# Rows of a and c from transposes of their columns, multiplied by g1 in VectorE's eviction; sums of squares of a as variances of these rows; positions redrawn

## The chip, the cores and the metric

The kernel runs on one core of one Trainium2 chip. The metric is the device time of one execution in microseconds, the median of three runs. A core has five engines with queues of their own, each worked through in order: TensorE (PE; its weight loads are shown as PEld), VectorE (DVE), ScalarE (ACT), GpSimd (POOL) and SyncE (SP, which issues the DMAs here).

## The reference

Two graph layers over 32 graphs of 512 nodes with 128 features. `adj` is sparse: about one entry in sixteen, and the diagonal.

```python
# layer 0: x1 = LN(x + Dinv (adj + I) Dinv (x W) + bias)
# layer 1, for each graph:
m_j = x1 @ W1[:D]                      # "a" in the kernel, centred over its features
m_i = x1 @ W1[D:]                      # "c" (with b1, centred)
pre = m_j[:, None, :] + m_i[:, :, None] + b1   # one row of 128 per pair of nodes (i, j)
msg = gelu(layernorm(pre) * g1 + be1)          # exact gelu
agg = einsum("bijo,bij->bio", msg, adj)
upd = layernorm(concat(x1, agg) @ W2 + b2) * g2 + be2
out = LN(x1 + upd)
```

With rows a and c centred, the sum of squares of a pair's row, which its layernorm needs, is sum(a^2) + sum(c^2) + 2 a.c. Only pairs with a non-zero entry in `adj` matter, and the kernel finds and computes just these.

## The kernel before

Everything named here is inside `sparse_path`. A batch is one graph, B = 32. Nodes lie in C = 4 chunks of 128, so `adj` has 16 blocks of 128x128. For each batch the kernel makes, per block and row, a list of the neighbours, and then works through 20 *units* (t, q): t = 0 to 3 are the first places of the lists, four units each, t = 4 and 5 the rest ("shared" places), two units each. A unit gathers the rows of its pairs with one-hot matmuls (`pairs`, into `u` in PSUM), adds the other row (`sums`, VectorE, L896; not for t >= 4), applies gelu with the pair's factor as scale (`messages`, ScalarE, L929), multiplies one-hot weights by `adj` (`weights`, GpSimd, L912 and L916, tile `sw`) and sums into `agg` (`aggregate`, TensorE, L943 and L953).

Around the units stand helpers that prepare the next batch and finish the last, written as generators whose steps end at `yield`:

- `layer0`: loads (`xs`, `a_nat`, `own_w`), layer 0, x1 and its transpose `x1t`; then `pat`, `pct` (L381, L383: the columns of a and c), `asq`, `csq`, `at`, `ct` out of them on ScalarE, the sums of squares `psq`, `pcs` on TensorE, and `key`, the 512x512 variances with a mask for absent edges: matmuls `pv` (L415, L416) and one VectorE eviction for each of four row chunks (L410). Last, the diagonal's own values: `own_p`, and `own_v` (L427).
- `lists` (VectorE, L519 and L523), `more` (L593, L596, L599), `factors`, `counts` (`over`, `count`, `count_h`, then `po` on TensorE, L634), `spots` (`up_to`, `pj`, `sj`), `sending` (`pl` on TensorE, `sent` on ScalarE, L686), `picks` (`rank` L706, `kept`, `picked` on VectorE, `r_s` on GpSimd): which neighbours, their variances, the overflow of long lists. `idx_d`, `idx_ds`, `sd_d`, `sd_ds` go out to DRAM and come back as `raw` and `sd_rows`; `raw` becomes the one-hot `s` (VectorE, L832) and its transpose `mt` (a transposing DMA, L840).
- `parts`: rows of a and c times g1 (`pac`, matmuls against `w1g`), copied to `ac` by ScalarE, b1's part added by GpSimd, and c split into three bf16 parts `c3`.
- `own_edges`, `finish` (`agg_sb`, `pu`, layernorms, the store).

The order of everything is written out by hand, in `PLAN`: for each step of each helper a position in half units, relative to the first unit of its batch; 40 positions are one batch, and -30 is 30 half units ahead. In the main loop each engine's instructions stand in the order in which the program issues them (the pairs of two units at even units, the aggregation of two units at odd ones, the steps of a position between). Before the first unit the framework's scheduler orders them. The transient PSUM tiles share one pool `ps` of three banks (`bank(...)`): a fourth tile waits until the engine that reads the first has done so.

Of the kernel before, what the change touches and what calls it, by code (L numbers as in the profile page):

```python
# [8 lines left out]
F32 = mybir.dt.float32  # L9
# [3 lines left out]
AF = mybir.ActivationFunctionType  # L13
ALU = mybir.AluOpType
# [4 lines left out]
P = 128  # L19
# [8 lines left out]
PAD = 4  # L28
NEG = -1e30
DEV = 12  # L30

PLAN = {
    "layer0": [-43, -41, -39, -39, -38, -37, -36, -34, -34, -33, -32, -31, -30, -30, -29, -28, -27, -27, -27, -27, -26, -24, -20, -18, -16, -3],
    "lists": [-26, -26, -25, -24, -23, -20, -19, -19, -18, -18, -14, -13, -13, -13, -12, -12, -12, -11, -11, -10, -10],
    "parts": [-20, -14, -12, -11, -6, -5, -4, -4, -4],
    "factors": [-12, -11, -10, -8, -7, -7, -7, -6, -5],
    "more": [-26, -25, -12, -10, -10, -10, -8, -7, -6, -6, -6, -5, -5, -5, -5, -5, -5, -5],
    "counts": [-3, -3, -2, -2, -2],
    "own_edges": [7, 18, 22, 30],
    "spots": [-2, -1, 0, 2, 3, 4, 6, 7, 7, 7],  # L40
    "sending": [8, 9, 9, 9, 9, 9, 9, 9, 9, 9, 9, 9, 9, 9, 9, 9, 9],
    "picks": [10, 12, 12, 14, 15, 18, 20, 20, 20, 20, 22, 23],
    "finish": [43, 44, 45, 50, 53, 55, 55, 60, 62, 69, 70, 79, 80],
}


def bcast(ap, n):

    return ap.unsqueeze(1).to_broadcast([ap.shape[0], n, ap.shape[-1]])
# [16 lines left out]
def sparse_path(ctx, tc, x, adj, w0, b0, w1, b1, g1, be1, w2, b2, g2, be2, out, most, flag):  # L66
# [37 lines left out]
    ident = const.tile([P, P], F32, name="ident")  # L104
# [1 line left out]
    ident_h = const.tile([P, P], BF16, name="ident_h")  # L106
    nc.vector.tensor_copy(ident_h, ident)
    ones = const.tile([P, P], F32, name="ones")
    nc.gpsimd.memset(ones, 1.0)

    stri = const.tile([P, P], BF16, name="stri")
    nc.gpsimd.memset(stri, 1.0)
# [33 lines left out]
    own = slice(0, C * C, C + 1)  # L146
# [12 lines left out]
    eps_t = const.tile([P, 1], F32, name="eps_t")  # L159
# [17 lines left out]
    bmean = const.tile([P, 1], F32, name="bmean")  # L177
    nc.vector.tensor_scalar(bmean, bsum, 1.0 / D, None, ALU.mult)
    b1c_col = const.tile([P, 1], F32, name="b1c_col")
    nc.vector.tensor_sub(b1c_col, b1_col, bmean)  # L180

    b1g = const.tile([P, D], F32, name="b1g")
    nc.vector.scalar_tensor_tensor(b1g, rows["b1"], bmean, rows["g1"], ALU.subtract, ALU.mult)
    w1g = const.tile([P, 2, D], F32, name="w1g")
    nc.vector.tensor_tensor(w1g, w1c, bcast(rows["g1"], 2), ALU.mult)


    parts = node.tile([P, 3, D], F32, tag="f0", name="be_parts")
# [66 lines left out]
    def bank(key):  # L255
        return ps.tile([P, 512], F32, tag="ps", name=key)
# [10 lines left out]
    def layer0(b):  # L267

        st = state[b] = {}
# [13 lines left out]
        pt = transposed(xs, f"x_{b}")  # L283
        yield
        for mc in range(C):
# [8 lines left out]
            pt = bank(f"pa_{b}_{mc}")  # L294
# [61 lines left out]
        pt = bank(f"pconv_{b}")  # L356
# [25 lines left out]
        pc = bank(f"pct_{b}")  # L382
        nc.tensor.matmul(pc, w1c[:, 1, :], x1t, start=True, stop=True)  # L383
        yield
        asq = node.tile([P, N], F32, tag="t1", name=f"asq_{b}")
        nc.scalar.activation(asq, pa, AF.Square)
        csq = node.tile([P, N], F32, tag="t3", name=f"csq_{b}")
        nc.scalar.activation(csq, pc, AF.Square, bias=b1c_col)
        yield
        at2 = node.tile([P, N], F32, tag="t0", name=f"at2_{b}")  # L390
        nc.scalar.activation(at2, pa, AF.Copy, scale=2.0)
        ct = node.tile([P, N], F32, tag="t2", name=f"ct_{b}")
        nc.scalar.activation(ct, pc, AF.Identity, bias=b1c_col)
        yield
        pa = bank(f"psq_{b}")
        for q in range(C):
            nc.tensor.matmul(pa[:, q : q + 1], asq[:, q * P : (q + 1) * P], ones[:, :1], start=True, stop=True)
# [10 lines left out]
        for q in range(C + 1):  # L408
            if q:
                nc.vector.scalar_tensor_tensor(  # L410
                    key[:, q - 1, :], pt, a_sum[:, q - 1 : q], c_sum, ALU.add, ALU.add
                )
# [18 lines left out]
    def parts(b):  # L431

        st = state[b]
        x1t = st["x1t"]

        ac = node.tile([P, C, 2, D], F32, tag="ac", name=f"ac_{b}", bufs=2)
        c3 = node.tile([P, 3, C, D], BF16, tag="c3", name=f"c3_{b}", bufs=2)
        for h in range(C // 2 + 1):
            if h:
                part = ac[:, 2 * h - 2 : 2 * h, :, :]  # L440
                nc.scalar.copy(part, pt.rearrange("p (c k d) -> p c k d", k=2, d=D))
            if h < C // 2:
                pt = bank(f"pac_{b}_{h}")
                for c in range(2):
                    n0 = (2 * h + c) * P
                    nc.tensor.matmul(
                        pt[:, 2 * c * P : 2 * (c + 1) * P], x1t[:, n0 : n0 + P], w1g, start=True, stop=True
                    )
            yield
        rest = ac[:, :, 1, :]  # L450
        nc.gpsimd.tensor_tensor(rest, rest, bcast(b1g, C), ALU.add)
# [8 lines left out]
        st["ac"], st["c3"], st["own"] = ac, c3, own_u  # L460

    def own_edges(b):

        st = state[b]
        var, u = st["own_v"], st["own"]
        nc.gpsimd.tensor_scalar(var, var, 0.0, 1.0 / D, ALU.max, ALU.mult)
# [81 lines left out]
    def factors(b):  # L548

        st = state[b]  # L550
        n_r = SLOTS * 2 * C * C
        sd = small.tile([P, n_r], F32, tag="sd", name=f"sd_{b}", bufs=1)
        by_c = sd.rearrange("p (t h c q) -> p h q c t", t=SLOTS, h=2, c=C)
        top = st["top"].rearrange("p (q c) h t -> p h q c t", c=C)
        for h in BOTH:
            nc.gpsimd.tensor_scalar(by_c[:, h], top[:, h, :, :, :SLOTS], 0.0, None, ALU.max)
        yield
        nc.scalar.activation(sd, sd, AF.Sqrt, bias=eps_t, scale=1.0 / D)
# [140 lines left out]
    def picks(b):  # L699
# [38 lines left out]
        for q in range(C):  # L738
# [2 lines left out]
        nc.gpsimd.tensor_scalar(  # L741
            ve.rearrange("p (k c q) -> p k q c", k=SHARED, c=C),
            picked[:, 1, :].rearrange("p (k q c) -> p k q c", k=SHARED, c=C),
            1.0 / D,
            EPS,
            ALU.mult,
            ALU.add,
# [594 lines left out]
```

## Time and profile before

| | |
|---|---|
| median of 3 runs | 2945.51 us (2942.2 to 2951.59) |
| the profiled execution | 2950.83 us, its span 2949.1 us, mean granted TensorE clock 0.987 |
| TensorE busy | 2780.1 us, 94% of the span |
| ScalarE | 2540.1 us, 86% |
| VectorE | 2441.2 us, 83% |
| GpSimd | 2132.8 us, 72% |
| HBM over the span | 57 GB/s |

Busy time is the time covered by an engine's instructions; TensorE's are pipelined and their ends modelled, so the time from one start to the next says more there than the duration of one. A group's row gives its line, engine, shapes and count, then busy time and mean duration of one, then the idle time of the engine just before it and what ended it. Rows of waits give total, number and longest. The chain that ended last follows only the last few microseconds of this kernel and is no guide to the rest.

### The profile page before, as it was taken

The page shows a single profiled execution, that of the slowest core. Times are in us where ns is not written, and L with a number is a line of the kernel's source. Part 1 is how long each engine was busy: PE and PEld are TensorE (multiplying, and loading weights), DVE is VectorE, ACT ScalarE, POOL GpSimd, SP SyncE. Part 2 cuts the span into 40 slices and gives each one's busy share as a digit, 9 for nine tenths or more (in the row PEclk, how much of TensorE's full clock was granted, in tenths as well). Part 3 has the DMA queues.
Part 4 walks back from the last instruction along what each step waited for, and adds up shares of the span by engine and source line. Part 5 has one row for each costly group of instructions (what it writes and reads, how often), then busy time and mean ns, then how long its engine had stood idle before and what let it go on. Part 6 is the DMA issues. An engine that isn't in the chain of part 4 may idle for free. (4 is left out here: it accounts for less than half of the span.)

```text
span 2949.1 us, 96041 instructions
## 1 busy us (share of the span) xinstructions
PE 2780.1 (94%) x35393; PEld 2314.2 (78%) x35393; DVE 2441.2 (83%) x9834; ACT 2540.1 (86%) x7841; POOL 2132.8 (72%) x2621
## 2 busy tenths in 40 slices
PE   4999999999999999999999999999999999999996
PEld 2788878788787788787888787788787888787885
DVE  5788988888988888988889888889888889888882
ACT  2888998888888888988888988888989888888885
POOL 3677877777877767776777777778777778776765
PEclk7999999999999999999999999999999999999998
DMA  1444444444443444434444434444434444434442
GB/s 43 91 93 105 103 101 79 99 91 107 106 97 75 93 99 102 109 82 89 100 102 102 101 79 99 93 108 103 101 79 99 89 109 106 100 79 96 91 97 48
DMA packets 593022, 276.09 MB, mean 94 GB/s; under 512 B 456112, under 2 KB 576048, under 8 KB 592544
## 3 DMA queue, kind: packets, MB, share of 16 engines
q1 hardware_dynamic: 592320, 269.41, 42.3%
q8 instruction: 281, 4.60, 0.6%
q14 instruction: 197, 1.61, 0.2%
q0 software_dynamic: 224, 0.46, 0.1%
HBM read 155.45 MB, written 13.63 MB: 57 GB/s over the span
## 5 line engine op out<-in xcount | busy, mean ns | idle before, releaser
L929 ACT ACTIVATE m<-m,r 128x128 f32<-128x128 f32 x4096 | 1267.4, 393 | 39.3 <-DVE m L896 39.3
L912 POOL TENSOR_TENSOR sw<-mt,a_t 128x512 f32<-128x512 bf16 x512 | 617.6, 1220 | 132.3 <-DMA mt<-s 74.1
L896 DVE TENSOR_TENSOR m<-u,ac 128x1024 f32<-128x1024 f32 x512 | 607.0, 1207 | 14.3 <-PE u L877 14.1
L943 PE MATMUL agg<-m,sw 128*64 128x128 f32 x8192 | 514.0, 277 | 5.6 <-ACT m L929 5.0
L943 PEld LDWEIGHTS agg<-m,sw 128*64 128x64 f32 x8192 | 442.7, 137 | 92.0 <-issue 45.5
L869 PEld LDWEIGHTS <-s 64*128 64x128 bf16 x12288 | 365.7, 95 | 138.3 <-issue 63.7
L869 PE MATMUL u<-c,s 64*128 64x128 bf16 x12288 | 434.0, 218 | 13.3 <-DVE s L832 12.7
L686 ACT COPY sent<-pl 128x328 f32<-128x328 f32 x512 | 221.4, 432 | 126.4 <-PE pl L690 66.9
L916 POOL TENSOR_TENSOR sw<-mt,sent 128x512 f32<-128x512 bf16 x256 | 291.3, 1161 | 9.0 <-PE agg L953 6.3
L690 PE MATMUL pl<-a_t,sj 128*128 128x164 f32 x2048 | 293.6, 304 | 0.0
L690 PEld LDWEIGHTS pl<-a_t,sj 128*128 128x128 f32 x2048 | 285.6, 190 | 8.5 <-DVE y L367 8.2
L929 ACT ACTIVATE m<-u,r_s 128x128 f32<-128x128 f32 x1024 | 279.0, 378 | 6.2 <-PE u L890 5.9
L884 PE MATMUL u<-ac,sj 128*128 128x128 f32 x2048 | 273.7, 277 | 0.0
L884 PEld LDWEIGHTS u<-ac,sj 128*128 128x128 f32 x2048 | 263.5, 191 | 12.0 <-DVE a_t L596 5.1
L953 PE MATMUL agg<-m,sw 128*128 128x128 f32 x2048 | 247.5, 277 | 0.0
L953 PEld LDWEIGHTS agg<-m,sw 128*128 128x128 f32 x2048 | 238.7, 192 | 9.2 <-POOL own_u L476 7.9
L887 PE MATMUL u<-c,s 128*128 128x128 bf16 x3072 | 213.3, 219 | 0.0
L523 DVE FIND_INDEX8 idx<-top,key 128x8 uint32<-128x64 f32 x1024 | 210.1, 218 | 0.0
L593 DVE MATCH_REPLACE8 key<-top,key 128x64 f32<-128x64 f32 x1024 | 205.0, 207 | 0.0
L741 POOL TENSOR_SCALAR ve_s<-picked 128x32 f32<-128x32 f32 x32 | 7.9, 248 | 262.0 <-DVE picked L727 262.0
L887 PEld LDWEIGHTS <-s 128*128 128x128 bf16 x3072 | 193.6, 98 | 3.0
L877 PE MATMUL u<-be_d,sd_rows 64*128 64x512 bf16 x1024 | 195.7, 378 | 0.0
(212 smaller groups left out, 5739.6 us busy)
## 6 DMA issues: line engine op xcount, KB each, us to landing
raw<-idx_d SPq DMA_DIRECT2D x256, 256.5 KB
raw<-idx_ds SPq DMA_DIRECT2D x64, 513.0 KB
a_nat<-in_adj_dram SPq DMA_DIRECT2D x32, 1024.0 KB
sd_rows<-sd_d SPq DMA_DIRECT2D x768, 12.0 KB
xs<-in_x_dram SPq DMA_DIRECT2D x32, 256.0 KB
out_dram<-o_sb SPq DMA_DIRECT2D x32, 256.0 KB
sd_d<-sd_p SPq DMA_DIRECT2D x256, 12.0 KB
mt<-s SPq DMA_TRANSPOSE x192
```

The source lines that it names most:

```text
L523: nc.vector.max_index(idx[:, to, h, :], top[:, to, h, :], half(to, h))
L686: nc.scalar.copy(sent[:, n - 1], pt[:, : SHARED * WIDE].rearrange("p (k w) -> p k w", w=WIDE))
L690: nc.tensor.matmul(pt[:, k * WIDE : (k + 1) * WIDE], sj[:, n, k * P : (k + 1) * P], at[:, n, :], start=True, stop=True,)
L869: nc.tensor.matmul(pu[:, h, c, :], s[halved(h), c, q * P : (q + 1) * P], c3[halved(h), k, c, :], start=(c == 0 and k == 0), stop=False,)
L884: nc.tensor.matmul(pu[:, h, c, :], place, st["ac"][:, q_h, 0, :], start=(c == 0), stop=False)
L887: nc.tensor.matmul(pu[:, h, c, :], s[:, c, q_h * P : (q_h + 1) * P], c3[:, k, c, :], start=False, stop=False)
L896: nc.vector.tensor_tensor(u.rearrange("p h c d -> p (h c) d"), pu.rearrange("p h c d -> p (h c) d"), bcast(state[b]["ac"][:, q, 0, :], 2 * C),
L912: nc.gpsimd.tensor_tensor(sw, mt[:, :, q, :], st["a_t"][:, q, :, :P], ALU.mult)
L916: nc.gpsimd.tensor_tensor(sw, mt[:, :, q_h, :], a, ALU.mult)
L929: nc.scalar.activation(m[:, h, c, :], u[:, h, c, :], AF.Gelu, scale=r[:, k : k + 1])
L943: nc.tensor.matmul(agg[halved(h), c, :], sw[0][:, c, halved(h)], m[:, h, c, :], start=(begin and c == 0), stop=(end and c == C - 1),)
L953: nc.tensor.matmul(agg[:, c, :], sw[h][:, c, :], m[:, h, c, :], start=False, stop=(end and h == 1 and c == C - 1),)
```

## The change

The columns of a and c (`at`, `ct`), which the kernel makes anyway for the variances, are transposed on TensorE into `pac` (eight transposes of 128x128, two banks), instead of multiplying x1t by W1 x g1. VectorE multiplies each bank by g1 on its way to `ac`, and takes bn_stats of the four unscaled rows of a out of the same bank; their variance takes the place of `asq`, `psq` and `a_sum`. So that all fits without another instruction, `at` is scaled by 2 x KEY, `ones` holds KEY = 32, the g1 of a is divided by 2 x KEY, and 1/D becomes 1/(KEY x D) in three places: `key` is 32 times what it was. b1 is in `ct` already, so GpSimd's addition goes. `parts` loses three steps, and all of `PLAN` has new positions: `parts` begins at 17 of the batch before instead of 20, the first key at 18 instead of 14, `counts` at 39 to 46 instead of 37 and 38, `own_v` at 5 of its own batch instead of 37 of the one before.

```diff
+KEY = 32.0
 PLAN = {
-    "layer0": [-43, -41, -39, -39, -38, -37, -36, -34, -34, -33, -32, -31, -30, -30, -29, -28, -27, -27, -27, -27, -26, -24, -20, -18, -16, -3],
-    "lists": [-26, -26, -25, -24, -23, -20, -19, -19, -18, -18, -14, -13, -13, -13, -12, -12, -12, -11, -11, -10, -10],
-    "parts": [-20, -14, -12, -11, -6, -5, -4, -4, -4],
-    "factors": [-12, -11, -10, -8, -7, -7, -7, -6, -5],
-    "more": [-26, -25, -12, -10, -10, -10, -8, -7, -6, -6, -6, -5, -5, -5, -5, -5, -5, -5],
-    "counts": [-3, -3, -2, -2, -2],
-    "own_edges": [7, 18, 22, 30],
-    "spots": [-2, -1, 0, 2, 3, 4, 6, 7, 7, 7],
-    "sending": [8, 9, 9, 9, 9, 9, 9, 9, 9, 9, 9, 9, 9, 9, 9, 9, 9],
-    "picks": [10, 12, 12, 14, 15, 18, 20, 20, 20, 20, 22, 23],
-    "finish": [43, 44, 45, 50, 53, 55, 55, 60, 62, 69, 70, 79, 80],
+    "layer0": [-41, -37, -36, -35, -35, -34, -32, -31, -30, -29, -29, -28, -28, -27, -26, -26, -25, -24, -23, -23, -22, -20, -17, -15, -12, 5],
+    "lists": [-21, -21, -20, -19, -17, -17, -17, -17, -17, -14, -12, -12, -12, -11, -11, -11, -11, -10, -10, -9, -8],
+    "parts": [-23, -23, -20, -14, -11, -7],
+    "factors": [-9, -9, -8, -8, -7, -7, -6, -6, -5],
+    "more": [-16, -9, -7, -7, -6, -6, -6, -5, -5, -4, -4, -3, -3, -3, -3, -3, -3, -3],
+    "counts": [-1, -1, 0, 1, 6],
+    "own_edges": [10, 11, 28, 35],
+    "spots": [1, 2, 3, 4, 5, 6, 8, 10, 10, 10],
+    "sending": [11, 11, 11, 11, 11, 11, 11, 11, 11, 11, 11, 11, 11, 11, 11, 11, 11],
+    "picks": [12, 16, 16, 17, 18, 19, 21, 21, 22, 22, 23, 23],
+    "finish": [45, 49, 49, 53, 56, 56, 60, 60, 68, 72, 75, 76, 84],
 }
...
-    nc.gpsimd.memset(ones, 1.0)
+    nc.gpsimd.memset(ones, KEY)
...
-    b1g = const.tile([P, D], F32, name="b1g")
-    nc.vector.scalar_tensor_tensor(b1g, rows["b1"], bmean, rows["g1"], ALU.subtract, ALU.mult)
-    w1g = const.tile([P, 2, D], F32, name="w1g")
-    nc.vector.tensor_tensor(w1g, w1c, bcast(rows["g1"], 2), ALU.mult)
+    g1_ac = const.tile([P, 2, D], F32, name="g1_ac")
+    nc.vector.tensor_scalar(g1_ac[:, 0, :], rows["g1"], 0.5 / KEY, None, ALU.mult)
+    nc.vector.tensor_copy(g1_ac[:, 1, :], rows["g1"])
...
     def layer0(b):
...
-        asq = node.tile([P, N], F32, tag="t1", name=f"asq_{b}")
-        nc.scalar.activation(asq, pa, AF.Square)
+        at = node.tile([P, N], F32, tag="t0", name=f"at_{b}")
+        nc.scalar.activation(at, pa, AF.Copy, scale=2.0 * KEY)
+        ct = node.tile([P, N], F32, tag="t2", name=f"ct_{b}")
+        nc.scalar.activation(ct, pc, AF.Identity, bias=b1c_col)
+        yield
         csq = node.tile([P, N], F32, tag="t3", name=f"csq_{b}")
         nc.scalar.activation(csq, pc, AF.Square, bias=b1c_col)
-        yield
-        at2 = node.tile([P, N], F32, tag="t0", name=f"at2_{b}")
-        nc.scalar.activation(at2, pa, AF.Copy, scale=2.0)
-        ct = node.tile([P, N], F32, tag="t2", name=f"ct_{b}")
-        nc.scalar.activation(ct, pc, AF.Identity, bias=b1c_col)
-        yield
-        pa = bank(f"psq_{b}")
-        for q in range(C):
-            nc.tensor.matmul(pa[:, q : q + 1], asq[:, q * P : (q + 1) * P], ones[:, :1], start=True, stop=True)
-        pc = bank(f"pcs_{b}")
-        nc.tensor.matmul(pc, ones, csq, start=True, stop=True)
-        yield
-        a_sum = small.tile([P, C], F32, tag="a_sum", name=f"a_sum_{b}")
-        nc.scalar.copy(a_sum, pa[:, :C])
+        ac = node.tile([P, C, 2, D], F32, tag="ac", name=f"ac_{b}", bufs=2)
+        st["ac"] = ac
+        stats = small.tile([P, C, 6], F32, tag="stats", name=f"stats_a_{b}")
+        a_var = small.tile([P, C, 2], F32, tag="a_var", name=f"a_var_{b}", bufs=1)
+        for h in range(C // 2 + 1):
+            if h:
+                parts_of = pt.rearrange("p (c k d) -> p c k d", k=2, d=D)
+                two = slice(2 * h - 2, 2 * h)
+                nc.vector.tensor_tensor(
+                    ac[:, two].rearrange("p c k d -> p c (k d)"),
+                    pt.rearrange("p (c e) -> p c e", e=2 * D),
+                    bcast(g1_ac.rearrange("p k d -> p (k d)"), 2),
+                    ALU.mult,
+                )
+                for c in range(2):
+                    nc.vector.bn_stats(stats[:, 2 * h - 2 + c, :], parts_of[:, c, 0, :])
+            if h < C // 2:
+                pt = bank(f"pac_{b}_{h}")
+                for c in range(2):
+                    here = slice((2 * h + c) * P, (2 * h + c + 1) * P)
+                    for k, cols in enumerate((at, ct)):
+                        n0 = (2 * c + k) * D
+                        nc.tensor.transpose(pt[:, n0 : n0 + D], cols[:, here], ident)
+                if h:
+                    pc = bank(f"pcs_{b}")
+                    nc.tensor.matmul(pc, ones, csq, start=True, stop=True)
+                yield
+        for c in range(C):
+            nc.vector.bn_aggr(a_var[:, c, :], stats[:, c, :])
         c_sum = node.tile([P, N], F32, tag="t1", name=f"c_sum_{b}")
         nc.scalar.copy(c_sum, pc)
...
 -                    key[:, q - 1, :], pt, a_sum[:, q - 1 : q], c_sum, ALU.add, ALU.add
+                    key[:, q - 1, :], pt, a_var[:, q - 1, 1:2], c_sum, ALU.add, ALU.add
...
-                nc.tensor.matmul(pt, at2[:, q * P : (q + 1) * P], ct, start=True, stop=False)
+                nc.tensor.matmul(pt, at[:, q * P : (q + 1) * P], ct, start=True, stop=False)
...
     def parts(b):
-        ac = node.tile([P, C, 2, D], F32, tag="ac", name=f"ac_{b}", bufs=2)
-        for h in range(C // 2 + 1):
-            if h:
-                part = ac[:, 2 * h - 2 : 2 * h, :, :]
-                nc.scalar.copy(part, pt.rearrange("p (c k d) -> p c k d", k=2, d=D))
-            if h < C // 2:
-                pt = bank(f"pac_{b}_{h}")
-                for c in range(2):
-                    n0 = (2 * h + c) * P
-                    nc.tensor.matmul(
-                        pt[:, 2 * c * P : 2 * (c + 1) * P], x1t[:, n0 : n0 + P], w1g, start=True, stop=True
-                    )
-            yield
         rest = ac[:, :, 1, :]
-        nc.gpsimd.tensor_tensor(rest, rest, bcast(b1g, C), ALU.add)
...
     own_edges, factors, picks: 1.0 / D becomes 1.0 / (KEY * D)
```

More of the change, by code (lines that the diff above doesn't have):

```diff
@@ L384, in layer0 @@
         yield
-        asq = node.tile([P, N], F32, tag="t1", name=f"asq_{b}")
-        nc.scalar.activation(asq, pa, AF.Square)
-        csq = node.tile([P, N], F32, tag="t3", name=f"csq_{b}")
-        nc.scalar.activation(csq, pc, AF.Square, bias=b1c_col)
-        yield
-        at2 = node.tile([P, N], F32, tag="t0", name=f"at2_{b}")
-        nc.scalar.activation(at2, pa, AF.Copy, scale=2.0)
+        at = node.tile([P, N], F32, tag="t0", name=f"at_{b}")
+        nc.scalar.activation(at, pa, AF.Copy, scale=2.0 * KEY)
         ct = node.tile([P, N], F32, tag="t2", name=f"ct_{b}")
@@ L394, in layer0 @@
         yield
-        pa = bank(f"psq_{b}")
-        for q in range(C):
-            nc.tensor.matmul(pa[:, q : q + 1], asq[:, q * P : (q + 1) * P], ones[:, :1], start=True, stop=True)
-        pc = bank(f"pcs_{b}")
-        nc.tensor.matmul(pc, ones, csq, start=True, stop=True)
-        yield
-        a_sum = small.tile([P, C], F32, tag="a_sum", name=f"a_sum_{b}")
-        nc.scalar.copy(a_sum, pa[:, :C])
+        csq = node.tile([P, N], F32, tag="t3", name=f"csq_{b}")
+        nc.scalar.activation(csq, pc, AF.Square, bias=b1c_col)
+        ac = node.tile([P, C, 2, D], F32, tag="ac", name=f"ac_{b}", bufs=2)
[27 more added lines that the diff above has]
+            nc.vector.bn_aggr(a_var[:, c, :], stats[:, c, :])
         c_sum = node.tile([P, N], F32, tag="t1", name=f"c_sum_{b}")
@@ L410, in layer0 @@
                 nc.vector.scalar_tensor_tensor(
-                    key[:, q - 1, :], pt, a_sum[:, q - 1 : q], c_sum, ALU.add, ALU.add
+                    key[:, q - 1, :], pt, a_var[:, q - 1, 1:2], c_sum, ALU.add, ALU.add
                 )
@@ L433, in parts @@
         st = state[b]
-        x1t = st["x1t"]
-        ac = node.tile([P, C, 2, D], F32, tag="ac", name=f"ac_{b}", bufs=2)
+        ac = st["ac"]
         c3 = node.tile([P, 3, C, D], BF16, tag="c3", name=f"c3_{b}", bufs=2)
-        for h in range(C // 2 + 1):
-            if h:
-                part = ac[:, 2 * h - 2 : 2 * h, :, :]
-                nc.scalar.copy(part, pt.rearrange("p (c k d) -> p c k d", k=2, d=D))
-            if h < C // 2:
-                pt = bank(f"pac_{b}_{h}")
-                for c in range(2):
-                    n0 = (2 * h + c) * P
-                    nc.tensor.matmul(
-                        pt[:, 2 * c * P : 2 * (c + 1) * P], x1t[:, n0 : n0 + P], w1g, start=True, stop=True
-                    )
-            yield
         rest = ac[:, :, 1, :]
-        nc.gpsimd.tensor_tensor(rest, rest, bcast(b1g, C), ALU.add)
         own_u = node.tile([P, C, D], F32, tag="own", name=f"own_u_{b}", bufs=2)
@@ L459, in parts @@
             yield
-        st["ac"], st["c3"], st["own"] = ac, c3, own_u
+        st["c3"], st["own"] = c3, own_u
     def own_edges(b):
@@ L465, in own_edges @@
         var, u = st["own_v"], st["own"]
-        nc.gpsimd.tensor_scalar(var, var, 0.0, 1.0 / D, ALU.max, ALU.mult)
+        nc.gpsimd.tensor_scalar(var, var, 0.0, 1.0 / (KEY * D), ALU.max, ALU.mult)
         nc.gpsimd.tensor_scalar(var, var, EPS, None, ALU.add)
@@ L557, in factors @@
         yield
-        nc.scalar.activation(sd, sd, AF.Sqrt, bias=eps_t, scale=1.0 / D)
+        nc.scalar.activation(sd, sd, AF.Sqrt, bias=eps_t, scale=1.0 / (KEY * D))
         yield
@@ L743, in picks @@
             picked[:, 1, :].rearrange("p (k q c) -> p k q c", k=SHARED, c=C),
-            1.0 / D,
+            1.0 / (KEY * D),
             EPS,
```

## The prediction, made before the changed kernel was run

> **What bounds the kernel now.** I read the page's busy shares first, then the list of waits, the timeline of one batch, and the windows cut where that timeline told me to.
>
> ```profile
> PE 2780.1 (94%) x35393; PEld 2314.2 (78%) x35393; DVE 2441.2 (83%) x9834; ACT 2540.1 (86%) x7841; POOL 2132.8 (72%) x2621
> ```
>
> The shares name TensorE, but VectorE's order decides where TensorE waits:
>
> ```profile
> DVE rank L706 <- ACT sent L686: 195.3, 32, 7.9
> DVE key L410 <- ACT m L929: 68.1, 31, 3.5
> PE po L634 <- DVE count_h L626: 31.6, 32, 1.0
> ```
>
> Once a batch VectorE stands 6.1 us for `sent`. From there it works almost without a pause until `count_h`, and there TensorE waits for it, 1.0 us each time. The line view of `count_h` gives the period:
>
> ```profile
> L626 DVE CAST count_h<-count x32: 174/174/175, 74.3 to 2839.2; 128x16 bf16<-128x16 f32 x32
> ```
>
> (2839.2 - 74.3) / 31 = 89.2 us. I cut one period in two: A from the start of `rank` to the end of `count_h`, B from there to the next `rank`. The windows (us, then busy us of TensorE, its weight loads, VectorE, ScalarE, GpSimd):
>
> ```profile
> 1000.60:1058.40 57.80, 55.61 (x748) 44.97 (x744) 54.35 (x258) 53.40 (x171) 46.11 (x49) 1.00 0.43 90
> 1058.40:1089.80 31.40, 29.94 (x354) 26.24 (x354) 22.09 (x48) 25.10 (x74) 19.43 (x33) 1.00 0.54 108
> ```
>
> In A TensorE and VectorE are nearly even. B is TensorE's: VectorE is idle for 9 of its 31 us. A gain must shorten VectorE's and TensorE's work in A, or TensorE's in B.
>
> **Prices.** These rows, from the line view by form, stand for what goes and comes:
>
> ```profile
> L446 PE MATMUL pac<-w1g,x1t 128*128 128x256 f32 x256 | 69.6, 394 | 1.6 <-DVE key L410 1.0 <-ACT ac L441 0.7
> L397 PE MATMUL psq<-ones,asq 128*128 128x1 f32 x256 | 34.3, 255 | 0.6 <-ACT asq L386 0.6
> L441 ACT COPY ac<-pac 128x512 f32<-128x512 f32 x64 | 36.2, 566 | 8.4 <-PE pac L446 8.4
> L451 POOL TENSOR_TENSOR ac<-ac,b1g 128x512 f32<-128x512 f32 x32 | 40.6, 1268 | 20.3 <-ACT ac L441 20.3
> L789 DVE TENSOR_TENSOR u<-pu,b_row 128x512 f32<-128x512 f32 x32 | 21.8, 680 | 3.3 <-PE pu L786 3.3
> ```
>
> *TensorE* loses `pac` (timeline 0.96 + 0.97 us) and `psq` (1.05), 2.98 a batch, and gains eight transposes. In the timeline four `pa` transposes start 0.44 us before what follows, four `pt_x` 0.54, so eight are 0.9 to 1.1, say 1.0. Net -2.0. [...] The row here has a mean of 278 ns for one, yet 73.5 us for 512, 144 ns each: they overlap, so I keep -2.0.
>
> *ScalarE* loses `asq` 0.58, `a_sum` 0.17 and two copies 1.13: -1.9. *GpSimd* loses the b1g addition: -1.3. Both are off the path in A (4 and 12 us idle there) and in B; I count nothing.
>
> *VectorE* gains two multiplications out of PSUM, four bn_stats, four bn_aggr. The row of the same form is L789, 680 ns; back to back such an instruction costs 0.61 to 0.72 from start to start (`agg_sb`, `u`), so 2 x 0.65 = 1.3. Four bn_stats from SBUF take 0.79 start to start, four bn_aggr 0.27. Sum +2.4 (sum of mean durations: 3.1). No row has bn_stats out of PSUM. Below: PSUM and SBUF sources cost the same in the nearest pair (L789 680, `kept` L721 686 ns). Above: as long as a multiplication of four times the length, 0.65 in place of 0.20, +1.8 a batch. I take the low end, being nearest in form. [...]
>
> Scaling by KEY and the constants cost nothing: operands of instructions that were there, or prologue.
>
> **Positions.** Counted in half units, 40 a batch. The order of the built program gives A's new contents. VectorE: the ten sums, four keys, lists and `more` stay; one gather `s` (1.2) now comes before `rank`, and `own_v` (0.6) goes to B. TensorE: a pair of `u` for the next batch's first units (1.9) comes in ahead of `po`, one aggregation (2.0) moves to B.
>
> *Stretch A.* VectorE's work: 54.35 + 2.4 - 1.2 - 0.6 = 54.95. TensorE's: 55.61 - 2.0 - 2.0 + 1.9 = 53.5. So VectorE sets A, plus the waits that it can't avoid. After `rank`, `chosen` and two sums (3.3 us) it needs `pu`: TensorE is there at 3.6, 0.3 idle. Up to the sum of (2,0) it has 8.1 us of work; TensorE has u 1.9, `pu` 1.9, `pt_x` 0.5, aggregation 2.0, `pat`/`pct` 1.9 and one u 0.9, less the 0.4 by which it starts early, 8.9: 0.8 idle. Then it needs `pac_0` at 10.5, being ready at 10.1: 0.4. Small gaps as now, 0.5. A = 54.95 + 0.3 + 0.8 + 0.4 + 0.5 = 57.0, against 57.8: **-0.8**. The key's present wait of 2.16 is what pays for most of the added work.
>
> The new wait is `pv_0`, which needs the bank that VectorE's bn_stats of `pac_0` releases (three banks; ScalarE released them before). It is free at 11.6; TensorE, with `pac` and `pcs`, comes at 12.0. Nothing, with 0.4 to spare. Behind a late `pv_0` stand `pidx_s` and the aggregation, and ScalarE's gelu is not held.
>
> At the end `po` now stands behind a pair of u (1.9 us), but VectorE is the later one, so TensorE still waits there or at `pidx`.
>
> *Stretch B.* TensorE 29.94 + 2.0 - 1.9 = 30.0. Of its 1.46 us of waits 0.57 is `pj` for `up_to`; that now follows a 3.7 us aggregation and goes. The others (pconv for ScalarE's `s`, 0.8) I keep: the masks hang on the load of `a_nat`. B = 30.9: **-0.5**.
>
> *Queues that steps are moved past.* On SP the loads of `xs`, `a_nat`, `own_w` go from 37 to 39, now behind the transposing DMA of `s` instead of ahead of it; `a_nat` waits in both for the last `more`, which ends 4.3 us before `count_h` does today and 2.5 then (a gather and `own_v` no longer lie between), so it lands 1.8 us later against `po`; TensorE asks for it 7 us after `po` instead of 4: no cost. The `idx_d` store goes from 30 to 32 with its reader at 34 unchanged, `idx_ds` from 18 to 19: the slack shrinks by 4.5 and 2.2 us; see the third rival. The store of `out` goes from 0 to 4 and nobody reads it. GpSimd's `r_s` (5.45 us) starts when `picked` is done, as now, and the two `sw` behind it are ready some 3 us before their aggregation.
>
> Sum: -1.3 us a batch, 31 full periods, -40; prologue and last batch 0 (the chain there gains the two evictions and loses `asq`, `psq`, `a_sum`; 3 us either way). The profiled execution took 2950.8 (span 2949.1), 5.3 above the median of the runs; 2910.5 on its scale, **2905** on the median's.
>
> **Rivals.** *VectorE's waits in A vanish too* (the four 0.3 to 0.8 waits are filled by queue depth, and B's): A 55.5, B 30.1, -3.6 a batch, 2834; half of it 2870. For: TensorE's own work in A is 53.5. Against: each wait is on an instruction that the order fixes. *Slower: PSUM reads on VectorE.* At 0.65 each four bn_stats cost 1.8 more, inside A, where every microsecond counts; -1.3 turns to +0.5, 2961. It decides from 0.33 us more per bn_stats (half of that if the multiplications suffer too). Against: the equal pair above. *No change: the stores.* If `s` on VectorE waits 1.3 us a batch for a raw row read back too early (now 14.7 us in all for `idx_ds`, 0.5 a batch), the gain is gone: 2945. That the change doesn't do what it says is excluded by the built order: `psq`, `asq` and the copies are absent.
>
> **How the numbers follow.** Forecast 0.53 (2874 to 2930, by -0.5 to -2.3 a batch), first rival 0.15, slower 0.20, no change 0.12. A measurement here tells apart about 0.3%, 9 us. Faster 0.53 + 0.15. The range leaves out the outer half of the first rival and the slow one's upper part: 2862 to 2958, of which the forecast's own range is the middle.
>
> **What would show it.** Period of `count_h` 87.9; A near 57.0 with VectorE over 54.5 busy; `key` no longer waiting 2 us; `pac` transposes near 140 ns each; bn_stats on `pac` near 280 ns. Wrong if bn_stats on `pac` is over 500 ns, if `pv_0` waits for VectorE by over 1 us, or if `s` waits for `raw`.

## The result, and the profile after

The changed kernel takes 3058.72 us (median of 6 runs, 3054.81 to 3060.3) against 2947.31 for the kernel before on the same chip: ratio 1.0378, 95% interval 1.0366 to 1.039. It is slower by 3.8%, where 2905 was forecast. The profiled execution has a span of 3054.8 us (2949.1 before) and a mean granted clock of 0.964 (0.987 before).

The page's busy shares of the kernel after:

```profile
PE 2785.6 (91%) x35137; PEld 2305.2 (75%) x35137; DVE 2498.4 (82%) x10154; ACT 2491.7 (82%) x7713; POOL 2075.6 (68%) x2589
```

TensorE has 256 instructions fewer and yet is busy 5.5 us longer: some of them ran slower, as the clock below shows. The line view of `count_h` gives the period, (2949.0 - 70.3) / 31 = 92.86 us in place of 89.19:

```profile
L629 DVE CAST count_h<-count x32: 174/174/176, 70.3 to 2949.0; 128x16 bf16<-128x16 f32 x32
```

The windows of one batch, cut as in the prediction (us, then busy us of TensorE, weight loads, VectorE, ScalarE, GpSimd; then granted clock, DMA share, GB/s):

```profile
1033.70:1089.30 55.60, 53.69 (x753) 42.90 (x747) 53.79 (x267) 51.35 (x164) 41.10 (x44) 1.00 0.31 70
1089.30:1127.60 38.30, 32.63 (x367) 28.55 (x363) 24.20 (x51) 26.56 (x79) 23.52 (x37) 0.91 0.54 118
```

A is shorter than forecast, B 7 us longer than the window of before, with TensorE idle for 5.7 of it and the clock down to 0.91. Over all batches (means, worked out from the records of `rank` and `count_h`):

| us a batch | A | B | period | clock at half, us in the whole run |
|---|---|---|---|---|
| before | 57.21 | 31.98 | 89.19 | 81 |
| after | 55.14 | 37.72 | 92.86 | 224 |

From here a change per batch is counted 31 times: 31 x 3.67 = 114 us, against 105.7 between the two spans (the prologue and the last batch became 4 us shorter each). Stretch A gave 2.1 us, stretch B took 5.7. In B TensorE is busy 33.1 us in the mean and idle 4.6; before, 30.8 and 1.2. The list of waits of the kernel after (waiting engine and line, what ended the wait, us in all, times, longest) names new ones:

```profile
DVE rank L709 <- ACT sent L689: 198.9, 32, 7.4
...
PEld pa L296 <- issue: 159.6, 80, 5.7
ACT m L932 <- DVE m L899: 133.7, 72, 3.4
DVE s L835 <- DMA raw<-idx_d: 125.3, 30, 6.0
PE pa L296 <- DVE sj L672: 107.2, 31, 5.3
...
PE pa L296 <- DMA a_nat<-in_adj_dram: 33.1, 24, 3.7
```

`rank` waits for `sent` as before, and `key` no longer waits for ScalarE. New are VectorE's 4 us a batch for raw rows, and TensorE's 3.5 us a batch in front of `pa` for a copy `sj` on VectorE. The timeline of one batch (its `count_h` ends at 994.43) shows that these are one chain. SP:

```profile
991.79 1.89 SPq L843 DMA_TRANSPOSE mt<-s  x1
993.78 1.03 SPq L271 DMA_DIRECT2D xs<-in_x_dram  x1
994.90 0.47 SPq L273 DMA_DIRECT2D a_nat<-in_adj_dram  x1
995.47 2.27 SPq L275 DMA_DIRECT2D own_w<-in_adj_dram  x1
997.79 1.25 SPq L826 DMA_DIRECT2D raw<-idx_d  x2
```

VectorE, and then TensorE, in the same batch:

```profile
1005.24 1.28 DVE L835 TENSOR_SCALAR s<-raw,node_h 128x2052 bf16<-128x2052 bf16 x1 [5.11 <-DMA raw<-idx_d]
1006.43 0.59 DVE L664 TENSOR_SCALAR up_to<-places,last 128x258 bf16<-128x258 bf16 x2
1006.94 0.68 DVE L672 COPY sj<-pj 128x512 f32<-128x512 f32 x1
```

```profile
1003.70 0.63 PE L296 MATMUL pa<-ident,a_nat 128*128 128x128 f32 x4 [1.74 <-DMA a_nat<-in_adj_dram]
1004.16 0.38 PE L677 MATMUL pj<-up_to,step_down 128*128 128x512 bf16 x1
1007.77 1.94 PE L296 MATMUL pa<-ident,a_nat 128*128 128x128 f32 x8 [3.23 <-DVE sj L672]
1009.53 0.61 PE L677 MATMUL pj<-up_to,step_down 128*128 128x512 bf16 x1
1010.07 3.63 PE L946 MATMUL agg<-m,sw 128*64 128x128 f32 x32
```

The window of the last three of these lines, with the columns as above (the granted clock is 0.50):

```profile
1007.70:1013.50 5.80, 5.73 (x41) 4.99 (x41) 5.58 (x10) 4.61 (x15) 0.82 (x4) 0.50 0.95 195
```

The gather `s` of t=1 stands at a fixed unit (half unit 4). VectorE was free for it at 5.7 us behind `count_h`, and the raw rows, issued at 3.4 behind `a_nat`'s 1 MB, were there at 10.8. The copy `sj` behind the gather frees one of TensorE's three banks, so eight transposes `pa` wait 3.23 us. Then the granted clock is 0.5: `pa` takes 1.94 us and the aggregation 3.63 (1.06 and 1.97 in before, where the granted clock is 1.00; the rows of e17 below show the same). Before, the rows were no earlier: in the batch whose `count_h` ended at 1058.26 they were issued 4.4 us behind it and the gather began at 11.0. But VectorE had more of B's steps to do ahead of the gather and waited 0.54 us. Over the batches the medians say the same: the gather begins 9.6 us behind `count_h`, with VectorE free for it at 5.7; before, it began at 10.3 with next to no wait.

### The profile page after: what moved, and what is told of

The parts are those of the page before. It is cut to its first block, busy times and chain, and to the rows that moved or that the text cites. A ratio compares the mean times of both kernels' runs of the same rounds, so it can differ in the third digit from the quotient of the medians.

```text
span 3054.8 us, 95936 instructions
## 1 busy us (share of the span) xinstructions
PE 2785.6 (91%) x35137; PEld 2305.2 (75%) x35137; DVE 2498.4 (82%) x10154; ACT 2491.7 (82%) x7713; POOL 2075.6 (68%) x2589
## 5 line engine op out<-in xcount | busy, mean ns | idle before, releaser
L899 DVE TENSOR_TENSOR m<-u,ac 128x1024 f32<-128x1024 f32 x512 | 617.1, 1211 | 29.5 <-PE u L880 20.0
L915 POOL TENSOR_TENSOR sw<-mt,a_t 128x512 f32<-128x512 bf16 x512 | 588.1, 1163 | 12.1 <-DMA mt<-s 9.0
L946 PE MATMUL agg<-m,sw 128*64 128x128 f32 x8192 | 542.5, 287 | 2.0 <-DVE agg_sb L778 2.0
L946 PEld LDWEIGHTS agg<-m,sw 128*64 128x64 f32 x8192 | 472.3, 144 | 82.0 <-issue 68.0
L887 PE MATMUL u<-ac,sj 128*128 128x128 f32 x2048 | 279.9, 280 | 43.8 <-DVE m L899 40.2
L835 DVE TENSOR_SCALAR s<-raw,node_h 128x2052 bf16<-128x2052 bf16 x128 | 161.8, 1264 | 130.6 <-DMA raw<-idx_d 125.3
L296 PE MATMUL pa<-ident,a_nat 128*128 128x128 f32 x512 | 98.1, 340 | 140.9 <-DVE sj L672 107.2
L241 POOL TENSOR_SCALAR ve_l<-mv_l 128x4 f32<-128x4 f32 x96 | 33.9, 353 | 249.8 <-DVE mv_l L238 249.8
```

The lines of the kernel that those rows point to most:

```text
L887: nc.tensor.matmul(pu[:, h, c, :], place, st["ac"][:, q_h, 0, :], start=(c == 0), stop=False)
L899: nc.vector.tensor_tensor(u.rearrange("p h c d -> p (h c) d"), pu.rearrange("p h c d -> p (h c) d"), bcast(state[b]["ac"][:, q, 0, :], 2 * C),
L915: nc.gpsimd.tensor_tensor(sw, mt[:, :, q, :], st["a_t"][:, q, :, :P], ALU.mult)
L946: nc.tensor.matmul(agg[halved(h), c, :], sw[0][:, c, halved(h)], m[:, h, c, :], start=(begin and c == 0), stop=(end and c == C - 1),)
```

## The experiments

The theories, as they came up; the expectations from e5 on name them so (in e1 to e4, theory 2 is VectorE's added evictions). 1: the raw rows of t=1 behind `a_nat` are the whole cause. 2: VectorE's order in B is, which puts other work ahead of the copies `sj` that free TensorE's banks. 3: raw rows and loads both have to be on their way before `count_h`. 4: VectorE comes too early to the gather. 5: the transfers crowded behind `count_h` are the cause.

All were timed against the kernel before. The ratio stands with its interval. Means over 31 batches, as above:

| run | us | ratio to before | A | B | period | half clock, us |
|---|---|---|---|---|---|---|
| e1_raw_early | 3067.8 | 1.0414 (1.0396 to 1.0431) | 55.12 | 38.02 | 93.14 | 201 |
| e2_arith_old_plan | 2976.5 | 1.0095 (1.0073 to 1.0117) | 57.58 | 32.55 | 90.14 | 87 |
| e3_plan_old_arith | 3181.2 | 1.0794 (1.0776 to 1.0812) | 59.10 | 37.75 | 96.85 | 260 |
| e4_loads_behind | 3012.9 | 1.0231 (1.0214 to 1.0248) | 55.10 | 36.31 | 91.41 | 114 |
| e5_raw_behind_dev | 3006.5 | 1.0202 (1.0172 to 1.0233) | 55.09 | 36.18 | 91.27 | 114 |
| e6_raw_and_order | 3009.8 | 1.0212 (1.0185 to 1.024) | 55.05 | 36.49 | 91.54 | 121 |
| e7_b_of_before | 3160.9 | 1.0722 (1.0687 to 1.0757) | 57.33 | 38.77 | 96.10 | 241 |
| e8_b_before_a_shifted | 3329.5 | 1.1306 (1.1273 to 1.1339) | 67.91 | 33.29 | 101.20 | 339 |
| e9_loads_ahead_too | 3071.0 | 1.0416 (1.0395 to 1.0437) | 55.17 | 38.02 | 93.19 | 225 |
| e10_out_early | 3043.4 | 1.0316 (1.0297 to 1.0335) | 55.14 | 37.59 | 92.73 | 217 |
| e11_spots_ahead | 3068.6 | 1.0422 (1.0387 to 1.0457) | 55.05 | 37.91 | 92.96 | 173 |
| e12_spots_and_raw | 3062.1 | 1.0382 (1.0343 to 1.0421) | 55.05 | 38.11 | 93.16 | 175 |
| e13_a_nat_apart | 3018.5 | 1.0234 (1.0217 to 1.0251) | 55.86 | 35.38 | 91.24 | 155 |
| e14_a_nat_and_raw | 2990.6 | 1.0129 (1.0111 to 1.0147) | 56.12 | 34.75 | 90.87 | 112 |
| e15_old_plan_a_nat | 2954.2 | 1.0016 (1.0006 to 1.0027) | 57.54 | 31.93 | 89.47 | 93 |
| e16_b_of_before_a_nat | 3050.5 | 1.0332 (1.0309 to 1.0355) | 58.21 | 34.55 | 92.76 | 163 |
| e17_all_loads_apart | 3012.7 | 1.021 (1.0196 to 1.0224) | 56.87 | 34.79 | 91.66 | 156 |
| e18_old_plan_loads_apart | 2944.2 | 0.9986 (0.9977 to 0.9995) | 57.60 | 31.46 | 89.06 | 71 |

### Arithmetic or positions: e2 and e3

The new arithmetic with the old PLAN (`parts` cut to its six steps), and the old arithmetic with the new PLAN:

```diff
# e2: arithmetic of after, every list of PLAN as before, but
+    "parts": [-11, -6, -5, -4, -4, -4],
# e3: arithmetic of before, every list of PLAN as after, but
+    "parts": [-25, -24, -23, -23, -23, -20, -14, -11, -7],
```

> The changed arithmetic with the positions of before (parts without its first three steps). Theory 1: the arithmetic is not at fault; the gather's wait for raw<-idx_d under 20 us, granted clock at least 0.98, time 2900 to 2965. Theory 2: time over 3000, with TensorE waiting for VectorE at pa or at the first pv for over 50 us.

> The arithmetic of before with the new positions (pac at -25, -24, -23, so that ac is ready for the new parts). Theory 1: the positions alone cost it; the gather's wait for raw<-idx_d over 60 us, B 36 to 39, granted clock under 0.975, time 3010 to 3090. Theory 2: time under 2970.

The loss in B belongs to the positions: 37.75 with the old arithmetic, 37.72 with the new. In these positions the arithmetic is a gain: A falls from 59.10 to 55.14. In the old positions it costs 1 us a batch. With the old arithmetic VectorE has no added evictions, so these are not the cause. Both times lie outside what was expected: e2 is 12 us above theory 1's range, e3 91 us.

### The raw rows of t=1: e1, e5 and e6

```diff
# e1: fetch(), ahead of the deviations of t=0; e5: behind them
         made_s[here] = gathers(*here, made_r[here])
+        if here[1] == 0:
+            made_r[here[0], 1] = gathered(here[0], 1)
         made_d[here] = deviations(*here)
...
-    if g + 3 in begins:
+    if g + 3 in begins and begins[g + 3][1] != 1:
# e6: e5, and
-    "layer0": [..., 5],    "finish": [45, ...]
+    "layer0": [..., 8],    "finish": [46, ...]
```

> The changed kernel with one DMA moved on SP: the raw rows of t = 1 are asked for right behind the gather of t = 0 (unit 18) instead of three units ahead (unit 21), so they stand in front of xs, a_nat and own_w. Theory 1 (the gather of t = 1 waits for raw rows queued behind the 1 MB of a_nat; VectorE stands, a PSUM bank is not freed, TensorE stands and its clock drops): the gather's wait for raw<-idx_d falls from 125 us to under 30, TensorE's wait at pa for sj from 107 to under 15, granted clock at least 0.98, stretch B from 37.4 to 31 to 33, time 2870 to 2910. Theory 2 (VectorE is late because of its added evictions, and would hold the bank anyway): B stays over 36, time 3020 to 3060.

> The changed kernel, with the raw rows of t=1 issued one fetch earlier as in e1_raw_early, but behind the deviation rows of t=0 in place of ahead of them. Theory 1 (the raw rows behind a_nat are the whole cause): e1 failed only by the late deviation rows, so here B falls from 37.7 to about 32 us a batch: 3058.7 - 31 x 5.7 = about 2885 us. Theory 2 (VectorE's order in B: sum, agg_sb and own_v stand ahead of the copies sj that free TensorE's banks): the wait for raw goes, TensorE still waits some 2 us a batch for sj and runs at half clock after it: 3000 to 3060 us.

> e5_raw_behind_dev, and agg_sb (finish 0) from position 45 to 46 and own_v (the last step of layer0) from 5 to 8, so that 1.3 us of VectorE's work no longer stands ahead of the copy sj at position 5. Theory 2: TensorE's wait for sj falls by about 1.3 us a batch and the half clock with it; B about 34, 2930 to 2980 us, at least 40 us below e5. Theory 1: within 15 us of e5.

VectorE's wait for `raw<-idx_d` is gone in all three. e1 gains nothing (9 us slower): the waits of e1 show the deviation rows, now behind 0.5 MB, and the banks again:

```profile
PE pj L677 <- DVE sj L672: 70.2, 32, 3.8
...
PE u L880 <- DMA sd_rows<-sd_d: 52.5, 57, 3.8
```

e5 puts that right and gives 52 us, not the 174 of theory 1: TensorE's wait for `sj` falls from 107 us to 16, but it then waits 57 us for `xs`. e6 is no faster than e5, so theory 2 fails in this form: `agg_sb` and `own_v` were not what TensorE waited for while `xs` was late.

### The loads: e4, e9 and e10

```diff
# e4
-    "layer0": [-41, ...
+    "layer0": [-38, ...
# e9: e5, and
+    "layer0": [-43, ...
-    "more": [..., -3, -3, -3, -3, -3, -3, -3],
+    "more": [..., -4, -4, -4, -4, -4, -4, -4],
# e10: e9, and
-    "finish": [..., 84],
+    "finish": [..., 80],
```

> The changed kernel with the loads of xs, a_nat and own_w three half units later (position 42 instead of 39), behind the raw rows of t = 1 on SP. Theory 1: the gather's wait for raw<-idx_d under 30 us; TensorE and ScalarE now wait for a_nat itself, some 2 to 3 us a batch more; B 33 to 36, time 2910 to 3010. Theory 2: B over 36, time 3020 to 3060 or more.

> e5_raw_behind_dev, with the last seven steps of more at position 36 in place of 37 and step 0 of layer0 (loads of xs, a_nat, own_w) at 37 in place of 39, so that on SP they come ahead of mt_0 again as before, behind the raw rows of t=1. Theory 3 (raw rows and a_nat both have to be on their way before count_h; e4 and e5 only traded one for the other): the loads start some 3.5 us earlier against count_h, TensorE's waits of e5 in B for xs and a_nat (1.6 + 0.8 + 0.5 us a batch) and the half clock behind them go; period about 88.3 in place of 91.3: about 2915 us, faster than before. Theory 2 (what is left is VectorE's order in B): within 20 us of e5, 2990 to 3015 us.

> e9_loads_ahead_too, with the last step of finish (o_sb and the store of out) at 80 in place of 84, so that the store no longer is what VectorE's agg_sb waits for (62 us in e5, 2 us a batch). Theory 2 (VectorE's order in B holds the banks): 1 us a batch or more comes off, 30 to 60 us below e9. Theory 3: TensorE has work without it, within 15 us of e9.

With the loads behind the raw rows (e4) TensorE waits for `xs`, 63 us; B, at 36.3, lies between the two theories' figures. With both ahead (e9) the transposing DMA of t=0 is the one that comes late. SP in e9 (`count_h` ends at 998.37):

```profile
995.85 1.23 SPq L826 DMA_DIRECT2D raw<-idx_d  x2
997.18 0.55 SPq L271 DMA_DIRECT2D xs<-in_x_dram  x1
997.83 0.45 SPq L273 DMA_DIRECT2D a_nat<-in_adj_dram  x1
998.37 0.45 SPq L275 DMA_DIRECT2D own_w<-in_adj_dram  x1
998.88 8.18 SPq L843 DMA_TRANSPOSE mt<-s  x1
```

The loads did start early, as meant, but the transposing DMA holds SP for 8.18 us in place of 1.89, GpSimd's `sw` waits 238 us in the run for `mt` (102 in e5), and all is given back. Theory 3 falls. e10 takes 28 us off e9, a little less than theory 2's 30 to 60, with B still at 37.6: VectorE's `agg_sb` waits 47 us in the run for the store of `out` in place of 120, but TensorE's `pj` now waits 83 us for `sj` in place of 3.

### Where the steps stand: e7, e8, e11 and e12

```diff
# e7 (A as after)
+    "layer0": [-42, -40, -39, -39, -38, -37, -36, -34, -33, -32, -30, ..., 0],
+    "counts": [-2, -2, -1, -1, -1],  "spots": [-1, 0, 1, 2, 3, 4, 6, 7, 7, 7],
+    "sending": [8, 9, ..., 9],  "picks": [11, ...],  "finish": [43, 44, 45, ..., 80],
# e8: layer0 0 to 9, own_v, counts, spots, sending, finish 0 to 2 and 12 as before;
#     every other position of after less 2
# e11
+    "layer0": [..., 1],  "counts": [-1, -1, 0, 0, 0],  "spots": [0, 0, 1, 2, 3, 3, 5, 6, 7, 7],
# e12: e11 with the edit of e5
```

> The changed kernel with its own positions in A, and B's steps (loads, layer0 1 to 9, counts, spots, sending, finish 0 to 2) near those of before; loads at 38. Theory 2 (positions in B are the loss, those in A the gain): A about 55.2, B about 32, period 87.2: 3058.7 - 31 x 5.7 = about 2885 us, below both kernels. Theory 1: the raw rows still come behind a_nat, with some 6 us between the two issues; where the load is still waited for, B stays above 35 and the time above 2970.

> The changed kernel with B's positions exactly as before and those of A all two half units earlier, so that loads and raw rows lie as before. Both theories: B about 32. If A's gain lies in the order of its steps among each other, A is about 55.2 and the time about 2885 us; if it lies in how they stand to the units (sums, gathers, aggregations), A is nearer to the 57.6 of e2_arith_old_plan: about 2960 us.

> The changed kernel, loads and raw rows untouched; VectorE's work that can stand ahead of the gather of t=1 is put there: counts 2 to 4 at 0, own_v at 1, spots at 0,0,1,2,3,3,5,6,7,7. Theory 4 (what changed is not the load but when VectorE comes to it: the trace has the gather 11.8 us behind count_h before and free for it at 5.7 after, raw landing at 10.8 there): VectorE comes about 4 us later to the gather, its wait falls from 4 to about 1 us a batch, the later copies sj no longer stand behind it, B falls from 37.7 to about 34: 3058.7 - 31 x 3.7 = about 2945 us. Rival (the transfers of B set its length, whatever VectorE does first): TensorE waits for xs, a_nat or mt instead, B stays above 36.5 and the time above 3020.

> e11_spots_ahead with the raw rows of t=1 fetched early as in e5_raw_behind_dev. Theory 4: with the wait already gone the raw rows ahead of xs and a_nat only delay these: slower than e11 by 10 to 60 us, about e5's 3006. Rival (transfers): like e5 within 15 us, 2990 to 3020, and e11 slower than that.

Theory 2 had e7 near 2885 us, theory 1 above 2970; it is on theory 1's side. e8, expected near 2885 or 2960, misses both by far. e7 asks for `a_nat` earlier than it can come: its load waits for the last reader of `key`, whose buffer it shares, and TensorE's `pa` waits 101 us in the run for it. e8 has B near before's (33.3), and its A is 10.7 us longer than before's; its list has new waits of `s` for both kinds of raw rows (178 us) and of TensorE's `u` for VectorE's `m` (161 us on the weight loads alone). Which of the moved steps starts that was not followed up. In e11 VectorE waits for no raw row (0.1 us before the gather in one batch), and nothing is gained: TensorE waits 85 us for `sj` at `pa` and stands 2.5 us there in that batch, now for a copy behind the gather, a sum and `agg_sb`. Its waits for `xs` and `a_nat` come to 10 us in the whole run, so with hardly a transfer waited for B is still 37.9. Theory 4 falls too. e12, with the raw rows early on top, is like e11 (their intervals overlap), though both sides had it near e5; TensorE's `pa` waits 82 us for `sj`.

### The transfers taken away: e13 to e18

`key` gets a buffer of its own, so that `a_nat` can be loaded at position 27, some 27 us ahead of `count_h` and of the transfers in B; e17 and e18 load `xs` there too.

```diff
-    key = big.tile([P, C, N], F32, tag="a_nat", ...)
+    key = big.tile([P, C, N], F32, tag="key", ...)
 def prepare(g):
+    b = (g + 53) // n_steps_b
+    if g >= 0 and (g + 53) % n_steps_b == 0 and b < B:
+        made_a[b] = loaded(b)      # tile and load of a_nat; in e17, e18 of xs too
 # layer0
+    a_nat = made_a.pop(b, None) or loaded(b)
# e13: after; e14: e5; e15: e2; e16: e7; e17: e14; e18: e15
# e17, e18 also: xs in the buffer t2, xb in that of xs and computed ahead of deg1
```

> The changed kernel, with a buffer of its own for key, so that a_nat needn't wait for the last reader of key: its load is issued at position 27, some 25 us ahead of count_h, all else in place. Theory 5 (the transfers behind count_h are the cause): the raw rows of t=1 land some 3 us earlier, the wait for them falls from 4 to about 1 us, TensorE's waits for sj and its half clock mostly go, B 33 or below: 3058.7 - 31 x 4.7 = about 2915 us. Rival (the positions of B are, through the order of VectorE and TensorE and the three banks): B stays above 36, 3000 us or more.

> e13_a_nat_apart with the raw rows of t=1 fetched early as in e5_raw_behind_dev. Theory 5: no wait for raw or a_nat is left, B about 32 as in before and A 55.1: about 2885 us, the best of all. Rival: 2990 us or more, like e5.

> e2_arith_old_plan (the new arithmetic in the old positions) with a_nat loaded early as in e13. There a_nat cost little (21 us of TensorE's wait, 55 of ScalarE's, in the whole run): both theories 2950 to 2975, 0 to 25 us below e2's 2976.5.

> e7_b_of_before with a_nat loaded early as in e13. Theory 5: e7's wait for a_nat (7 us a batch) goes, with it the half clock; B about 32, A 55 to 57: 2885 to 2945 us, below e13. Rival: 3050 us or more.

> e14_a_nat_and_raw with xs loaded at position 27 too (xs in the buffer t2, xb in that of xs, xb computed ahead of deg1). Theory 5 (the transfers behind count_h are the cause): TensorE's 2.2 us for xs go, B about 32.5, A 56: 2990.6 - 31 x 2.2 = about 2920 us, below before. Rival (the order of the steps is the rest): the 2.2 us come back as waits for sj or for ScalarE, 2975 us or more.

> e15_old_plan_a_nat with xs loaded at position 27 too. TensorE waits there 0.6 us a batch for pt_x (17 us in the run): 2954.2 - 17 = about 2937 us, just below before; where VectorE's count_h is what is late, no change, 2950 to 2958. Theory 5 has e17 below this one by 10 us or more, the rival above it.

e13 and e14 take 40 and 68 us off, where theory 5 wanted 144 and 174. In e13 VectorE's wait for `raw<-idx_d` falls from 125 us to 12, as theory 5 said, but TensorE's `pj` now waits 70 us for `sj`. e16 is 110 us faster than e7, its wait for `a_nat` being gone, but with A at 58.2 and B at 34.6 it is as far from theory 5's figure and stands at the rival's 3050; TensorE's 50 us of waits for `sj` at `pconv` are in both. In e14 no raw row and no `a_nat` is waited for in B, and TensorE's largest gap in the batch shown is `xs`:

```profile
990.43 0.66 PE L262 MATMUL pt_x<-ident,xs 128*128 128x128 f32 x4 [2.18 <-DMA xs<-in_x_dram]
```

e17 takes that away as well. The kernel becomes 22 us slower than e14, for A grows, but it shows what the rest of B is: TensorE no longer waits for any load there, and B stays at 34.79. The same microseconds are idle a little later (line numbers are 7 higher here). TensorE and VectorE in one batch of e17:

```profile
998.78 1.06 PE L303 MATMUL pa<-ident,a_nat 128*128 128x128 f32 x8 [0.34 <-DVE sj L679]
1002.12 0.39 PE L684 MATMUL pj<-up_to,step_down 128*128 128x512 bf16 x1 [2.27 <-DVE sj L679]
1002.44 1.97 PE L953 MATMUL agg<-m,sw 128*64 128x128 f32 x32
```

```profile
997.95 0.68 DVE L679 COPY sj<-pj 128x512 f32<-128x512 f32 x1
998.55 1.22 DVE L906 TENSOR_TENSOR m<-u,ac 128x1024 f32<-128x1024 f32 x1
999.68 0.68 DVE L785 TENSOR_TENSOR agg_sb<-agg,own_u 128x512 f32<-128x512 f32 x1
1000.28 0.68 DVE L452 TENSOR_REDUCE own_v<-own_p 128x4 f32<-128x512 f32 x1
1000.87 0.59 DVE L671 TENSOR_SCALAR up_to<-places,last 128x258 bf16<-128x258 bf16 x2
1001.38 0.68 DVE L679 COPY sj<-pj 128x512 f32<-128x512 f32 x1
```

`pj` needs a bank and gets it from a copy `sj` that stands behind a sum, `agg_sb` and `own_v`: 2.3 us of VectorE's work in program order, TensorE idle 2.27. The lists of waits of e17 and of e18, in the old positions, have this for the whole run:

```profile
PE pj L684 <- DVE sj L679: 68.7, 31, 2.3
PE pj L684 <- DVE sj L679: 0.6, 1, 0.6
```

So the transfers and the positions each hold a part of the loss. B goes from 37.72 to 34.79 by the transfers (2.9, with the raw rows asked for early), and from 34.79 to the 31.46 of e18, which has the old positions with the same arithmetic and the same loads out of the way (3.3). Of the 3.3 this wait is 2.2. The shares depend on the order of counting: in the old positions, from e2 to e18, the loads are worth only 1.1. These are differences of whole runs, and the half clock is in both: B has 86 us of it in e17 and 6 in e18, an estimated 1.3 us a batch at most. That it is the steps ahead of `sj`, and no other position that differs, is read from the trace and not tried by a run. A rises in e17 to 56.87: 1.25 MB now pass there, and `s` waits 68 us for `raw<-idx_ds` in place of 11.

e15 came out as expected, e18 between its two figures; e17 lies above it by 68 us, on the rival's side. The new arithmetic in the old positions, with these loads apart, takes 2944.2 us, 0.1% under the kernel before. It is the fastest kernel of this study, and its lead is below what a reader should build on. Not tried: e6's moves on top of e17, and the old arithmetic with the loads apart.

## Why the prediction was wrong

*TensorE -2.0, right.* Eight transposes from the first start to the start of what follows take 0.93 us in 31 of the 32 batches (2.11 in the first), 116 ns each, under the 140 of the row that stood for them. The mean duration of one is 276 to 290 ns in the same trace: they overlap.

*VectorE +2.4, right.* The rows by form in the kernel after:

```profile
L400 DVE TENSOR_TENSOR ac<-pac,g_ac 128x512 f32<-128x512 f32 x64 | 43.6, 681 | 18.0 <-PE pac L414 18.0
...
L407 DVE BATCH_NORM_STATS2 stats_a<-pac 128x6 f32<-128x128 f32 x128 | 31.0, 283 | 0.0
...
L420 DVE BATCH_NORM_AGGREGATE a_var<-stats_a 128x2 f32<-128x6 f32 x128 | 11.5, 150 | 0.0
...
L621 DVE TENSOR_SCALAR over<-a_t 128x256 bf16<-128x256 f32 x32 | 9.4, 293 | 0.0
```

The multiplication takes 681 ns (680 in the row that stood for it), bn_stats out of PSUM 283 ns (280 named as the sign); the durations sum to 3.1 us a batch, as the prediction had it. The slower rival on PSUM reads is refuted: its point of decision was 0.33 us more.

*Stretch A -0.8, measured -2.1.* The mechanism held; two terms were too dear. `over` costs 0.29 us in place of a mean of 1.67, which takes VectorE's 54.95 to 53.57; its mean over the stretches A is 53.58. The waits came to 1.6 us (55.14 - 53.58) in place of 2.0. One of these was summed wrongly: TensorE's terms up to the sum of (2,0) make 8.7 and not 8.9, so 0.6 us idle and not 0.8. That `over` would be shorter was not foreseen, so this part of A's gain is luck. A is what the first rival said, 55.5; its B is not.

*Stretch B -0.5, measured +5.7: the step that failed.* It was worked out as TensorE's work, 30.0, plus its old waits, 0.9, and its queue step ended with "no cost". In the runs TensorE is busy 33.1 us there and idle 4.6. (The 0.57 us of `pj` for `up_to` did go: 17.3 us in the whole run before, 3.5 after.) Three things were missing. I compared when loads were issued and when TensorE asked for `a_nat`, and did not ask what stands behind them on SP: the raw rows of t=1, for which VectorE now waits 4 us a batch. (`a_nat` itself is issued 3.2 us later against `count_h` by the medians, not 1.8.) I did not count how much of B's work VectorE has ahead of the gather of t=1, which stayed at its unit while `spots`, `counts` and `own_v` moved behind it (11 us before, 5.7 after). And I gave TensorE's wait for VectorE's `sj`, 3.5 us a batch, no price, though three banks serve `spots` and `layer0` alike; in the new order the copies stand behind sums, `agg_sb` and `own_v`. The half clock came on top: 143 us more of it, all in the stretches B, at most 72 us of work lost. That is 2.3 us a batch by an estimate that takes all of it as busy, as much as TensorE's busy time in B grew (30.8 to 33.1).

*The rivals.* "No change: the stores" had the right kind of wait, `s` for raw rows, but for another store (`idx_ds`) and at 1.3 us. The sign named for a wrong prediction, `s` waiting for `raw`, is what happened, at 4 us. That wait is not the sole cause: e1 and e5 remove it and e11 leaves 12 us of it; e1 and e11 are 9 and 10 us slower than the changed kernel, e5 is 52 us faster.

*Sum.* Had B kept before's 31.98, A alone would have given a period of 87.1, below the forecast 87.9. No run here has both.

## What to carry to other kernels

When steps are moved on in-order queues, follow each shared buffer from the engine that frees it: list what now stands ahead of the freeing instruction, including fixed work that was not moved. A stretch with several late parties (loads, raw rows, a transposing DMA, banks) gives back little when one of them is mended (here 52 us of 111 at best, in e5); take all of one kind away at once, and see which microseconds stay. And price an idle TensorE above its own length, since the clock may follow (0.50 for 6.8 us from within an idle 3.23 us, in the first batch shown above).

## What the runs showed of the hardware

- Between 100 and 2900 us of the run the granted clock fell to 0.5 in 30 stretches after (17 of 3.4 us, 12 of 6.8, one of 10.2) against 2 before (3.4 and 6.8). Of TensorE's 33 idle times of 3 us and more in the whole run after, 31 have such a stretch beginning inside them or within 2 us behind them; of the 7 between 2.0 and 2.5 us 4 have, of the 19 between 1.0 and 1.5 us none. In e17 it happened at 26 of the 32 idle times of 2.0 to 2.5 us. That the idle time brings the fall is read from these counts; no run tries it by itself.
- The same `over` on VectorE took 1.42 to 1.83 us in the 31 batches of before where GpSimd was at work beside it, and 0.27 to 0.30 us in the 32 of after and the one of before where it was not. In e2 most took 0.98 to 1.00 us: there one `sw` of GpSimd, begun 0.3 us earlier, runs beside it, and `over` ends 0.15 us behind that `sw`; in before it ends as much behind the second of two. That GpSimd's instruction is what holds `over` back is the author's reading of these times, and no run tries it by itself.
- A transposing DMA held SP for a median of 1.9 us in after, where the loads come behind it on the queue. Right behind the 1.3 MB of the loads it held SP for 4.1 to 7.1 us (before, 30 batches), and behind 1.8 MB for 6.1 to 8.2 us (e9, 30 batches).
